# A four-layer graph network in float32: T^T by VectorE, logits and T products in larger batches, z shifted instead of W2 centred, and setup sums moved off TensorE

## Chip, cores and metric

One core of one Trainium2 chip. The metric is the time of one execution on the device, in microseconds (us); medians of several executions are given. All timed runs quoted are of the fast state. "TensorE's clock" is the clock that the throttle granted, 1.00 at full speed.

## The reference, cut to what matters

`x` is 128 graphs of 64 nodes and 512 features, that is 8192 tokens in float32, `adj` the 128 weighted adjacency matrices. Four layers follow, each as `x = x + layer(relu(layernorm(x)), adj)`:

```python
# layer 0: hypergraph convolution 512 -> 1024, relu, layer norm, convolution 1024 -> 512, plus its own input
h = relu(hypergraph_conv(x, adj, W1, b1)); h = layer_norm(h, gamma, beta)
y = hypergraph_conv(h, adj, W2, b2) + x
# layer 1: graph attention with s = (x @ w) @ a, tanh, leaky relu, exp; A @ x @ w
# layer 2: dense attention over the 64 nodes of a graph
query, keyt, value = x @ Wq.T + bq, x @ Wk.T + bk, x @ Wv.T + bv
weight = adj * exp(query @ keyt.T); out = (weight / weight.sum(2)) @ value
# layer 3: diffusion with a transition matrix T from attention
e = leaky_relu(sj[None, :] + si[:, None] + ab); T = normalised(adj * exp(e))
H = sum over k = 0..2 of (T^k @ x) @ Wk[k] + bk[k]; out = relu(H)
```

Some parts of the weights can be worked out once, ahead of the tokens ("setup"): Wq^T Wk for the logits and its bias row, the bias row beta W2 of layer 0, and three vectors (w a, and the two halves of Wv aw) that are then needed in every partition ("spread").

## The kernel before, cut

The kernel works on 16 groups of 512 tokens: first layers 0 and 1 for all groups (first stage), then layers 2 and 3 (second stage). Large products use a seven-product scheme (Strassen's), so VectorE forms sums of blocks beside TensorE. The program first lists all operations, with a cost each, and a list scheduler inside the kernel's own source then fixes the order on each engine. Every transfer goes through one queue, issued by SyncE:

```python
class Graph:
    ENGINES = ("PE", "DVE", "ACT", "POOL", "SP")
    LATENCY = {"PE": 0.30, "DVE": 0.12, "ACT": 0.12, "POOL": 0.15, "SP": 2.0}
    ...
            end = t + o.cost + self.LATENCY[o.eng]      # SP: every transfer is taken to land 2 us after its issue
...
STRETCH, PERIOD1, PERIOD2 = (2.01, 1.52, 3.8, 3.15), 99.32, 100.99
AT = {"x0": -1000.31, "apart": -0.04, "w1": -1140.59, ...}   # priorities of the parts, fitted to that model
```

The parts that the change touches:

```python
def setup_l0():                     # beta W2, and W2 centred: column sums on TensorE
    def mm():
        for c in range(KH):
            nc.tensor.matmul(p.t[0:2, :], gsc[:, c, :], w2_sb[:, c, :], start=(c == 0), stop=(c == KH - 1))
    ...                             # two products that copy the two rows into all partitions (pm, pb)
    for c in range(KH):             # w2 = w2 * gamma - pm
        dve(0.75, ...scalar_tensor_tensor(w2_sb[:, c, :], w2_sb[:, c, :], gb2[:, 0, c:c + 1], pm.t, ...))

def spread(col, dst, r, key):       # a [128, 4] column -> 512 values in every partition
    dve(0.69, lambda: nc.vector.tensor_mul(quad(dg), ident[:, None, :]..., col()[:, :, None]...), r, [dg])
    pe(c_mm(512, 1), lambda: nc.tensor.matmul(p.t, ones, dg.t, start=True, stop=True), [dg], [p])
    act(0.6, lambda: nc.scalar.copy(dst(), p.t), [p], [key])

def dot(in0, in1, acc, r, w):       # a row of h times a spread vector, summed
    j = Buf("o")
    dve(0.77, ...scalar_tensor_tensor(j.t, in0(), 1.0, in1(), ..., accum_out=acc()))

# layer 2: logits of one half as soon as its query block is there: 16 records of 64 columns
pe(c_mm(64, 4), mm, ...)
# layer 3: T^T by TensorE and identity, then T^2, then T products of one tile at a time
for t in range(T):
    nc.tensor.transpose(quad(pt)[:, t, :], tr.t[:, t, :], ident)
act(0.59, lambda: nc.scalar.copy(tt.t[:, :, 0, :], quad(pt)), [pt], [(tt, 0)])
```

## Time and profile before

| | before |
|---|---|
| time, median of 3 runs | 2398.47 us (2397.96 to 2401.6) |
| span of the profiled run, TensorE's clock | 2395.1 us, 0.998 |
| TensorE busy / idle | 2356.3 us / 38.8 us |
| VectorE, ScalarE, GpSimd busy | 1721.2, 1263.5, 938.2 us |
| period (time from one group to the next), first / second stage | 71.77 / 73.20 us |

TensorE is busy 98% of the span. The profile's lines for this, and what follows from them, are shown in the prediction.

### The profile page before, as it was taken

Reading aid. Unit: us, or ns where it says so; the run is one execution under the profiler, and the core shown is the slowest. Engines: PE = TensorE matmul, PEld = TensorE weight load, DVE = VectorE, ACT = ScalarE, POOL = GpSimd, SP = SyncE. Lnnn points to the kernel's source line nnn. Section 1 sums busy time; section 2 is a strip of 40 time slices with the busy share of each in tenths; the row PEclk is TensorE's granted clock in tenths of the full one; section 3 lists DMA queues with packets and bytes.
Section 4 is the critical chain, followed back from the end, with each engine's and each line's share of the span. In section 5 each row is a group of like instructions: output and inputs, shape, how many; then the busy total and the mean of one; then the engine's idle time right before and its main releaser. Section 6 shows DMA issues by size and latency. Waiting matters only on the chain.

```text
span 2395.1 us, 33543 instructions
## 1 busy us (share of the span) xinstructions
PE 2356.3 (98%) x11930; PEld 1855.0 (77%) x11930; DVE 1721.2 (72%) x3676; ACT 1263.5 (53%) x1754; POOL 938.2 (39%) x1450
## 2 busy tenths in 40 slices
PE   7999999999999999999999999999999999999999
PEld 3576677776777776777778888888888888888887
DVE  7887878787878787877878556666666666666664
ACT  2666565566565566565745445544445444454431
POOL 5234455434455434455344333333333333333321
PEclk9999999999999999999999999999999999999999
DMA  7232222232223222222532232222322222222211
GB/s 242 54 80 47 65 68 71 68 78 51 65 66 73 67 80 52 61 67 77 146 89 62 66 74 55 69 56 58 78 64 60 66 50 71 73 56 64 52 42 36
DMA packets 335928, 168.78 MB, mean 70 GB/s; under 512 B 284688, under 2 KB 290832, under 8 KB 335760
## 3 DMA queue, kind: packets, MB, share of 16 engines
q1 hardware_dynamic: 335760, 166.63, 28.0%
q8 instruction: 94, 1.54, 0.3%
q14 instruction: 74, 0.61, 0.1%
HBM read 64.76 MB, written 34.70 MB: 42 GB/s over the span
## 4 chain that ended last, share of the span: by engine, by line
PE 84%; DVE 6%; DMA 4%; ACT 2%; POOL 2%; issue 2%; SPq 0%; DVEq 0%; POOLq 0%; ACTq 0%
PE ps L595 60%; PE ps L818 11%; PE ps L534 4%; PE ps L936 2%; PE ps L731 2%; PE ps L879 2%; DVE s_s_vu_tt L869 1%; DMA x<-xm 1%; PE ps L844 1%; ACT o L543 1%; DVE bd L854 1%; ACT h L525 1%; POOL u L867 1%; POOL rs L511 1%; DVE st L508 1%
## 5 line engine op out<-in xcount | busy, mean ns | idle before, releaser
L525 ACT ACTIVATE h<-x,nm,rs 128x512 f32<-128x512 f32 x384 | 307.1, 813 | 456.5 <-POOL nm L518 455.3
L595 PE MATMUL ps<-wb_mem,rT_a 128*128 128x256 f32 x2056 | 476.8, 380 | 1.7 <-DVE z_hT L615 0.9
L595 PEld LDWEIGHTS ps<-wb_mem,rT_a 128*128 128x128 f32 x2056 | 386.5, 190 | 74.8 <-issue 20.3
L510 POOL TENSOR_SCALAR rs<-mv 128x1 f32<-128x1 f32 x320 | 101.5, 317 | 534.2 <-DVE mv L509 452.9
L595 PE MATMUL ps<-wb_mem,s_s_vu_tt 128*128 128x256 f32 x1152 | 275.0, 379 | 0.2 <-DVE s_s_vu_tt L587 0.2
L595 PE MATMUL ps<-wb_mem,tmp_mB_s 128*128 128x256 f32 x1152 | 261.3, 379 | 0.2 <-DVE tmp_mB_s L587 0.2
L595 PEld LDWEIGHTS ps<-wb_mem,s_s_vu_tt 128*128 128x128 f32 x1152 | 218.5, 190 | 43.1 <-issue 10.5
L595 PE MATMUL ps<-wb_mem,mT_a 128*128 128x256 f32 x1016 | 240.7, 380 | 1.8 <-ACT u L563 1.3
L595 PEld LDWEIGHTS ps<-wb_mem,tmp_mB_s 128*128 128x128 f32 x1152 | 217.6, 190 | 29.6 <-DVE tmp_mB_s L587 0.6
L595 PE MATMUL ps<-wa_mem,mT_a 128*128 128x512 f32 x512 | 238.0, 593 | 2.1 <-DVE u L567 2.1
L949 POOL TENSOR_TENSOR u<-u,bk_b 128x256 f32<-128x256 f32 x96 | 76.2, 799 | 352.3 <-DVE u L567 292.6
L511 POOL TENSOR_TENSOR rs<-rs,mhalf 128x1 f32<-128x1 f32 x320 | 202.9, 634 | 26.6
L595 PEld LDWEIGHTS ps<-wb_mem,mT_a 128*128 128x128 f32 x1016 | 190.6, 190 | 28.6 <-ACT u L563 1.5
L508 DVE BATCH_NORM_STATS2 st<-x 128x6 f32<-128x512 f32 x256 | 174.1, 680 | 32.4 <-DMA x<-xm 30.8
L595 PE MATMUL ps<-wa_mem,s_s_vu_tt 128*128 128x512 f32 x384 | 182.9, 599 | 1.0 <-ACT c_b L453 0.6
L595 PEld LDWEIGHTS ps<-wa_mem,mT_a 128*128 128x128 f32 x512 | 96.0, 190 | 105.4 <-issue 92.5
L565 DVE TENSOR_TENSOR u<-ps,u 128x256 f32<-128x256 f32 (+1 forms) x160 | 84.4, 527 | 112.1 <-PE ps L595 84.6
L623 POOL TENSOR_TENSOR u<-u,row_sh_q 128x256 f32<-128x256 f32 x96 | 70.9, 746 | 235.0 <-DVE u L565 205.9
L545 ACT COPY rT_a<-z_hT 128x1024 uint16<-128x1024 uint16 x128 | 144.3, 1161 | 4.4 <-DMA z_hT<-tmp_mB_s 4.2
L534 PEld LDWEIGHTS ps<-bd,h 128*128 128x128 f32 x1024 | 129.0, 192 | 16.1 <-issue 8.6
L707 ACT ACTIVATE z_hT<-z_hT 128x512 f32<-128x512 f32 x128 | 79.8, 625 | 116.7 <-DVE z_hT L615 116.6
L563 ACT COPY u<-ps 128x256 f32<-128x256 f32 (+1 forms) x160 | 72.5, 453 | 129.7 <-PE ps L818 71.5
(172 smaller groups left out, 4317.1 us busy)
## 6 DMA issues: line engine op xcount, KB each, us to landing
x<-in_x_dram SPq DMA_DIRECT2D x64, 256.0 KB, 2.8
xm<-x SPq DMA_DIRECT2D x64, 256.0 KB, 2.0
x<-xm SPq DMA_DIRECT2D x64, 256.0 KB, 2.7
out_dram<-x SPq DMA_DIRECT2D x64, 256.0 KB, 2.2
adj<-in_adj_dram SPq DMA_DIRECT2D x32, 256.0 KB, 4.1
rw<-row SPq DMA_DIRECT2D x96, 64.0 KB, 2.8
wb_mem<-in_Wk_dram SPq DMA_DIRECT2D x6, 512.0 KB, 4.4
wa_mem<-in_W1T_dram SPq DMA_DIRECT2D x2, 1024.0 KB, 5.9
```

What stands on the lines that cost most here:

```text
L508: dve(0.69, lambda i=i: nc.vector.bn_stats(st.t[:, i, :], src(i)), [r[i]], [(st, i)])
L510: pool(0.3, lambda: nc.gpsimd.tensor_scalar_add(rs.t, mv.t[:, 1:2], EPS), [mv], [rs])
L511: pool(0.65, lambda: nc.gpsimd.tensor_tensor(rs.t, rs.t, mhalf, ALU.pow), [rs], [rs])
L525: act(0.82, lambda: nc.scalar.activation(h.t, xx.t, AF.Relu, bias=nm.t, scale=rs.t), [xx, nm, rs], [h])
L534: nc.tensor.matmul(quad(p)[:, c, :], h.t[:, c * P:(c + 1) * P], rhs(), start=True, stop=True)
L545: act(1.16, lambda: nc.scalar.copy(u16(dst()).rearrange("p c (k q) -> p c k q", q=2), u16(back()).rearrange("p (q c r) -> p c r q", q=2, c ...
L563: act(n / 1200 + 0.17, lambda: nc.scalar.copy(at(0)(), p1.t[:, :n]), [p1], [(U, 0)])
L565: dve(c_v(n), lambda: nc.vector.tensor_add(at(1)(), p2.t[:, :n], at(0)()), [p2, (U, 0)], [(U, 1)])
L595: nc.tensor.matmul(p.t[:, :n], lhs()[:, c, :], rhs(c), start=first and c == 0, stop=c == kc - 1, skip_group_check=True)
L707: act(0.63, lambda: nc.scalar.activation(z.t[:, cols], z.t[:, cols], AF.Relu), [(z, j)], [(z, j)])
L818: nc.tensor.matmul(pair(p.t)[:, o, :], a, b, start=first and o == 0 and c == 0, stop=c == 1, skip_group_check=True)
L949: pool(0.88, lambda: nc.gpsimd.tensor_add(U.t[:, iv], U.t[:, u[1]], add()), [u, ka], [v])
```

## The change

Its intent: take from TensorE what other engines or the queue can do (the transposes of T, the sums in setup, the spreads), batch narrow products so that TensorE changes less often between narrow and full blocks (a full block took 1.92 us between two narrow ones and 1.73 among its own kind), and fit the order anew. The diff, cut to its core:

```diff
-    STRETCH, PERIOD1, PERIOD2 = (2.01, 1.52, 3.8, 3.15), 99.32, 100.99
+    STRETCH, PERIOD1, PERIOD2 = (2.14, 5.21, 2.77, 0.81), 82.23, 144.68
     AT = { ... all offsets new, seven added for the ends of the stages, "last" dropped ... }
 def setup_l0():
-    (column sums of W2 on TensorE, W2 centred by VectorE)
+        acc, pb = Buf("o"), Buf("ps")
+        for c in range(KH):      # beta W2 by VectorE: first c by tensor_scalar, then
+                dve(0.77, lambda c=c: nc.vector.scalar_tensor_tensor(
+                    acc.t, w2_sb[:, c, :], gb2[:, 1, c:c + 1], acc.t, op0=ALU.mult, op1=ALU.add), ...)
+        for c in range(KH):      # W2 * gamma by ScalarE
+            act(0.72, lambda c=c: nc.scalar.activation(w2_sb[:, c, :], w2_sb[:, c, :], AF.Copy, scale=gb2[:, 0, c:c + 1]), ...)
 def spread(col, dst, r, key):
-    (diagonal by VectorE, product with ones by TensorE, copy by ScalarE)
+        d = dram.tile([KD, P], F32, name=f"spread{len(spreads)}")
+        dma(4, lambda: nc.sync.dma_start(d.rearrange("c p -> p c"), col()), r, [k])
+        dma(256, lambda: nc.sync.dma_start(dst(), d.rearrange("c p -> (c p)").partition_broadcast(P)), [k], [key])
 def setup_l2():                  # key bias: Wk^T bq
-            (4 products of one column for each of 4 tiles of Wk)
+                dve(0.77, ...scalar_tensor_tensor(bk.t, k_.t, bq_c[:, o:o + 1], bk.t, ...))   # then 4 products at the end
 layer 0:                         # z shifted by its mean, W2 no longer centred
-    act(0.7, ...activation(half(), half(), AF.Copy, scale=rs.t))
+    nm = offset(mv, rs)          # GpSimd
+    act(0.72, ...activation(half(), half(), AF.Identity, bias=nm.t, scale=rs.t))
 layer 2:                         # logits of two query blocks together
-    pe(c_mm(64, 4), mm, ...)
+    pe(1.5, mm, ...)             # 32 records
 layer 3:
-    nc.tensor.transpose(quad(pt)[:, t, :], tr.t[:, t, :], ident); act copy
+    nc.vector.transpose(tt.t[... 32 rows ...], tr.t[... 32 columns ...])     # 8 a group
-    pe(c_mm(128, KD) + 0.2, lm, ...)            # T products of one tile
+    pe(2 * c_mm(128, KD) + 0.25, lm, ...)       # of two tiles, four PSUM banks
```

## The prediction

> **What bounds the kernel now.** I read the engine totals and the 40 slices first, then busy time by stretches, TensorE's groups by form, TensorE's waits, and TensorE's timeline of one steady period.
>
> ```profile
> PE 2356.3 (98%) x11930; PEld 1855.0 (77%) x11930; DVE 1721.2 (72%) x3676; ACT 1263.5 (53%) x1754; POOL 938.2 (39%) x1450
> PE   7999999999999999999999999999999999999999
> DVE  7887878787878787877878556666666666666664
> ...
> 0.00:20.00 20.00, 10.48 (x24) 5.06 (x25) 10.66 (x23) 2.10 (x2) 5.04 (x15) 1.00 0.78 279
> ...
> 400.00:640.00 240.00, 240.00 (x1000) 170.85 (x999) 189.92 (x420) 149.19 (x210) 113.18 (x176) 1.00 0.26 65
> ...
> 1180.00:1240.00 60.00, 55.22 (x312) 45.73 (x311) 40.02 (x85) 23.43 (x33) 21.07 (x37) 1.00 0.48 130
> ...
> 1640.00:1880.00 240.00, 239.06 (x1441) 205.90 (x1440) 153.03 (x313) 110.96 (x150) 83.02 (x128) 1.00 0.27 65
> ```
>
> The columns of the stretches are length, then busy time of TensorE, weight load, VectorE, ScalarE, GpSimd, then clock and DMA. TensorE has work without a gap in both long stages; VectorE, the next, is busy 79% of the first (layers 0 and 1) and 64% of the second (layers 2 and 3). Of the 2395.1 us, 38.8 are idle on TensorE: 16.6 in the first 100 us (9.5 of them before the first matmul), 9.9 at the handover between stages (1150 to 1290), some 7.6 in the last 105 us, and the rest are 0.3 us waits. So only two things change the time: TensorE's own work, and these gaps.
>
> Busy time of matmuls overlaps in this profile, so I cost by start-to-start distance. The recurring order of instructions gives 71.77 us a group of 512 tokens in the first stage (230.81 to 302.58 in the chain) and 73.20 in the second (1330.76 to 1403.95); the 16 groups make 1148 and 1171 us, and 76 us are left for setup, edges and gaps.
>
> ```profile
> L844 PE MATMUL ps<-y_qT,z_hT 128*64 128x64 f32 x1024 | 44.7, 231 | 1.4 <-ACT y_qT L830 1.3
> L915 PE MATMUL ps<-ident,bd 128*128 128x128 f32 x64 | 9.8, 275 | 1.9 <-DVE bd L908 1.9
> L435 PE MATMUL ps<-wb_mem,gsc 128*2 128x512 f32 x16 | 7.0, 592 | 0.0
> L474 PE MATMUL ps<-bq_c,tmp_mB_s 128*128 128x1 f32 x32 | 3.7, 242 | 0.0
> L452 PE MATMUL ps<-tmp_mB_s,ones 128*128 128x512 f32 x6 | 3.2, 622 | 0.1
> ```
>
> These are the groups that the change touches: logits, transposes of T, and three setup products. An ordinary matmul counts as two records here. The next lines are TensorE's timeline, first in the steady second stage and then once at the handover:
>
> ```profile
> 1645.35 3.62 PE L818 MATMUL ps<-row_sh_q,wa_mem 128*128 128x256 f32 x16
> 1648.89 0.69 PE L844 MATMUL ps<-y_qT,z_hT 128*64 128x64 f32 x16
> 1649.51 1.99 PE L818 MATMUL ps<-wa_mem,row_sh_q 128*128 128x256 f32 x8
> 1651.43 0.69 PE L844 MATMUL ps<-y_qT,z_hT 128*64 128x64 f32 x16
> 1652.05 1.99 PE L818 MATMUL ps<-z_hT,wa_mem 128*128 128x256 f32 x8
> ...
> 1205.82 1.89 PE L818 MATMUL ps<-wa_mem,row_sh_q 128*128 128x256 f32 x8
> 1207.64 1.15 PE L844 MATMUL ps<-y_qT,z_hT 128*64 128x64 f32 x32
> 1208.72 1.99 PE L818 MATMUL ps<-z_hT,wa_mem 128*128 128x256 f32 x8
> 1210.55 1.89 PE L818 MATMUL ps<-wa_mem,row_sh_q 128*128 128x256 f32 x8
> ```
>
> A block of 8 products of 256 columns takes 1.73 us from start to start among its own kind (1669.07 to 1670.80), but 1.92 between two blocks of logits. A switch into and out of a narrow block therefore costs 0.19 us outside the block, besides something inside it.
>
> [...] the trace has 216 ns a record for 256 columns of float32, [...] and I use 216. [...] No VectorE transpose is in this trace.
>
> **The change part by part.**
> Transposes of T: four records at 1614.17, the next kind at 1614.61, so 0.44 us a group go from TensorE, in 16 groups 7.0 us. ScalarE loses one 0.585 us eviction a group. VectorE gains eight transposes of 32 rows by 128: its 512 and 256 column operations take 0.69 and 0.42 us, so 128 columns should take 0.28, together 2.3 us a group (an estimate). That raises it from 64% to 67%: beside the path.
>
> Second power of T: half the columns, but 65 columns (8 records in 0.84 us at 485.67) cost nearly what 128 do (0.89): nothing gained.
>
> Logits in pairs: one block of 16 records costs 0.62 + 0.19 = 0.81 us, one of 32 costs 1.08 + 0.19 = 1.27. A pair saves 0.35. In steady state all four of a group stood apart, so 0.70 a group, 11 us in all, less a little for the groups where they already touched.
>
> T products in pairs of tiles: a block of 16 records takes 1.09 us, of 32 1.98, of 48 2.88, that is 0.9 for each 16 and 0.19 for a block. But the scheduler already placed them as 16 + 48 in each group; 32 + 32 is two blocks too. No gain, and four PSUM banks are held at once.
>
> Setup: column sums of W2 (L435) 6.96 us from start to start, one selecting product 0.96 and the 0.69 wait for its row; the key bias has 32 records at 0.11, of which 8 stay, minus 2.6; the three spreads minus 2.6. That is 13.1 us of work and 0.7 of wait, replaced by two transfers a spread, about 8 VectorE operations more for the bias row and key bias, and 8 ScalarE scalings of W2.
>
> z shifted instead of W2 centred: 64 more GpSimd operations of 0.466 us, 30 us beside a queue at 49%; the shift is the bias of an activation that ran anyway. It adds 0.5 us of latency before each pair of transposed tiles, which other layers' work covers in the long stages.
>
> New order: the first stage's 71.77 us are already TensorE's work without a gap (its products add up to 71.6), so no schedule can gain there. At the ends it can: the Wq and Wk tiles now go ahead of W1, and W2 far later. Before, the first matmul waited to 9.5 us for Wk behind 2 MB of W1, with DMA 78 to 96% busy; with only 1 MB ahead I estimate 5 us. Handover and tail have new offsets of their own; I give them 4 and 1, and 1 for the 15 waits of 0.3 us for the reciprocal.
>
> The sum: 7.0 + 11 + 13.1 + 0.7 = 31.8 of work; plus about 10 of gaps; less 1 to 2 for a hole that the freed setup work leaves while VectorE, over 90% busy between 40 and 80 us, still prepares the first tiles. 2398.5 minus about 41 is **2357 us**.
>
> **The rivals.**
> A, *the setup gain evaporates*: TensorE waits at 63, 74 and 84 us for VectorE, not for itself; if VectorE sets the end of setup, the 13 us removed there turn into idle time and VectorE's added operations lengthen it. For it: VectorE's load between 40 and 80 us. Against: from 28 us the combined tiles were ready, and setup products ran to 41.9 in front of the first layer product. Then about 2369.
> B, *the edges gain more*: with the offsets searched anew for start, handover and end, most of the 34 us at the edges close to half. For it: the added offsets aim at just that, and there is mixed work to fill with. Against: the first loads and the last chain cannot be hidden. Then about 2345.
> C, *a new wait in the second stage*: paired logits hold both query buffers and delay two PSUM evictions, paired T products need four banks. If each group gains one 0.7 us wait, the logit gain is gone: about 2368. Against it: TensorE always has two layers' work to choose from there.
>
> **Range and chances.** The mechanical part (transposes, logits, setup) is 32 us, and I hold it to within 6; the edges are worth 0 to 22. So 2340 to 2374 eight times in ten. The limit for faster by over 2% is 2350.5, some 7 us below my centre, reached if B holds: 0.33. Slower by over 2% would need 48 us of new waits where TensorE has none: 0.01. Within 2%: 0.66.
>
> **What would show it.** Right: no record of an identity transpose; about 32 logit blocks of 32 records each, two a group; a second-stage period of 72.1 us against 73.2 and a first-stage period of 71.8 as before; first matmul near 5 us; idle time of TensorE near 29 us. VectorE's transposes at about 0.28 us. Wrong: a second-stage period still at 73, then C; idle time in the first 100 us above 20 us, then A; idle time in all under 20 us, then B. Most likely to spoil the figure is the size of the gaps at the edges, which comes from a schedule that I can't see.

## The result and the profile after

| | before | after |
|---|---|---|
| time, median (runs, same rounds) | 2400.03 us (4) | 2410.00 us (4; 2409.17 to 2411.19) |
| span of the profiled run, clock | 2395.1 us, 0.998 | 2409.4 us, 0.989 |
| TensorE busy / idle | 2356.3 / 38.8 us | 2337.8 / 71.6 us |

The ratio is 1.0041, with a 95% interval of 1.0024 to 1.0058. A ratio here is the mean time of one kernel's fast runs over the mean of the other's of the same rounds, so it is not quite the ratio of the medians. The change costs some 10 us where I had predicted a gain of 41. TensorE did lose work, and lost more to waiting.

From the page of after, the totals and the slices:

```profile
PE 2337.8 (97%) x11818; PEld 1851.6 (77%) x11818; DVE 1763.9 (73%) x3801; ACT 1267.6 (53%) x1742; POOL 965.9 (40%) x1514
...
PE   7689999999999999999999999999999999999998
...
DVE  7778878877888787787867667766667766667763
```

The hole is in slices 2 and 3, that is between 60 and 180 us, where before had 9s. To say how much each stage gives or takes, I compare the moments at which the same products start in both traces:

| from ... to | before | after | difference |
|---|---|---|---|
| start to the 16th group's product of the first stage with the adjacency | 1059.8 us | 1085.7 | +25.9 |
| to the second group's T squared | 264.3 | 266.0 | +1.6 |
| to the 15th group's (13 periods) | 952.7 | 934.6 | -18.1 |
| to the 16th group's | 69.2 | 73.8 | +4.6 |
| to the end | 49.1 | 49.4 | +0.3 |

The differences are taken before rounding; their sum, +14.3, is the difference of the two spans. **The second stage gained as intended, and the start of the program lost more.** The period of the first stage is 71.77 us in both, so nearly all of the 25.9 arises before about 180 us.

The second stage first. TensorE's groups by form of after (busy time in us and mean ns):

```profile
L850 PE MATMUL ps<-y_qT,z_hT 128*64 128x64 f32 x1024 | 37.3, 225 | 1.6 <-DVE y_qT L835 1.6
...
L932 PE MATMUL ps<-s_s_vu_tt,bd 128*128 128x64 f32 x128 | 18.0, 288 | 8.5 <-DVE s_s_vu_tt L923 8.5
```

The identity transposes are gone. The logits take 37.3 us of busy time in place of 44.7. TensorE's timeline of a steady stretch of after (start, length, then line and operands):

```profile
1744.81 1.15 PE L850 MATMUL ps<-y_qT,z_hT 128*64 128x64 f32 x32
1745.89 1.99 PE L817 MATMUL ps<-z_hT,wa_mem 128*128 128x256 f32 x8
1747.72 1.89 PE L817 MATMUL ps<-wa_mem,row_sh_q 128*128 128x256 f32 x8
1749.54 1.15 PE L850 MATMUL ps<-y_qT,z_hT 128*64 128x64 f32 x32
```

Two blocks of 32 records a group, 1.08 us each from start to start, as predicted.

Now the start. The stretches of after (length; busy TensorE, weight load, VectorE, ScalarE, GpSimd; clock, DMA share, GB/s):

```profile
0.00:20.00 20.00, 10.61 (x24) 5.02 (x24) 7.08 (x25) 1.65 (x2) 4.68 (x16) 1.00 0.83 292
20.00:40.00 20.00, 14.35 (x46) 7.52 (x46) 19.65 (x17) 10.73 (x17) 18.07 (x14) 0.91 0.67 231
40.00:60.00 20.00, 19.36 (x51) 9.40 (x51) 16.82 (x29) 6.13 (x11) 1.57 (x4) 0.83 0.50 173
60.00:80.00 20.00, 9.54 (x31) 4.72 (x29) 13.64 (x38) 8.80 (x11) 6.45 (x16) 0.93 0.73 65
80.00:100.00 20.00, 12.40 (x47) 9.16 (x48) 13.38 (x21) 8.21 (x11) 9.08 (x7) 0.81 0.59 128
```

TensorE is idle 100 - 66.26 = 33.7 us of the first 100, against 16.6 before. The granted clock falls as well, to 0.81 between 80 and 100 us. TensorE's timeline of after (in brackets: idle before, and what ended it):

```profile
72.16 1.99 PE L593 MATMUL ps<-wb_mem,rT_a 128*128 128x256 f32 x8 [2.94 <-ACT rT_a L543]
83.75 3.78 PE L593 MATMUL ps<-wb_mem,rT_a 128*128 128x256 f32 x8 [9.60 <-ACT u L561]
```

After the hole of 2.94 us a block of 8 records takes its usual 1.99 us, at a granted clock of 1.00 (72.16 to 73.90 us); after the one of 9.60 it takes 3.78, at 0.50 (83.75 to 87.50 us). So more was lost there than the hole's own length: the block behind it took 1.79 us longer.

What TensorE waited for in after, in all the run (total us, times, longest):

```profile
PE ps L593 <- ACT u L561: 9.6, 1, 9.6
PE ps L593 <- DVE mT_a L585: 8.8, 1, 8.8
PE ps L932 <- DVE s_s_vu_tt L923: 8.5, 2, 6.8
PE ps L459 <- DMA tmp_mB_s<-in_Wk_dram: 7.1, 1, 7.1
...
PE ps L434 <- DVE o L430: 4.3, 1, 4.3
```

The first is said to wait for ScalarE. What kept ScalarE? Its own timeline says: a transposing transfer.

```profile
82.14 1.16 ACT L543 COPY rT_a<-z_hT 128x1024 uint16<-128x1024 uint16 x1 [9.09 <-DMA z_hT<-tmp_mB_s]
83.32 0.37 ACT L561 COPY u<-ps 128x256 f32<-128x256 f32 x1
```

And the timeline of the queue that issues all transfers at that time:

```profile
69.22 0.48 SPq L442 DMA_DIRECT2D spread<-col  x1
69.80 0.48 SPq L319 DMA_DIRECT2D tmp_mB_s<-in_aw_dram  x1
70.39 3.21 SPq L542 DMA_TRANSPOSE z_hT<-tmp_mB_s  x2
80.30 0.33 SPq L443 DMA_DIRECT2D c_b<-spread  x1
80.69 1.24 SPq L542 DMA_TRANSPOSE z_hT<-tmp_mB_s  x1
```

The spread is written at 69.22 and read back at 80.30, as soon as the write has landed; until then the queue stands still. It is tempting to say that the transposing transfer behind the read-back was what ScalarE lacked. But that one, issued at 80.69, landed only at 86.44, after ScalarE had gone on at 82.14. ScalarE had waited for the transfer issued at 70.39, before the queue stood still, which landed at 82.12. The transposing transfers of this stretch, with their times from issue to landing (minimum/median/maximum), first in after, then in f6, a run described below in which, up to this point, only the layout of the spread's write differs:

```profile
L542 SPq DMA_TRANSPOSE z_hT<-tmp_mB_s x3: 1295/1352/1823, 67.7 to 71.8; - x3
DMA to landing us min/median/max: 3.2/10.6/11.7
```

```profile
z_hT<-tmp_mB_s SPq DMA_TRANSPOSE x2, 4.0
```

The transfer issued just before the write took 3.2 us; a load of 256 KB issued right behind it took 11.4, and the two transposing transfers after that 11.7 and 10.6. In f6 that load takes 3.6 and those two 4.0 in the median. So transfers that were in flight together with this write landed late, then ScalarE went on late, then TensorE. What in the write holds the others up, no run shows. The spread's transfers by name, and the queue's own waits, in after:

```profile
spread<-col SPq DMA_DIRECT2D x3, 2.0 KB, 10.9
```

```profile
SPq L443 <- DMA spread<-col: 25.0, 3, 10.3
```

Three writes of 2 KB land after 10.9 us in the median, and the queue stands for 25.0 us in all. The write goes to `d.rearrange("c p -> p c")`, so neighbouring elements of the source lie 512 bytes apart in memory: 512 pieces of 4 bytes. The packet counts agree: the queue moved 338496 packets in after and 337344 in f6, which writes 128 pieces of 16 bytes, and the 1152 between them are 3 x (512 - 128). Other transfers of the same 2 KB (`row<-col`) land after 1.4 us.

The second wait in the list (8.8 us, for VectorE) has the same root by another way: there VectorE waits for the write and then for its read-back. VectorE's timeline of after at the third spread, 150 us into the run:

```profile
138.70 0.37 DVE L585 TENSOR_TENSOR s_s_vu_tt<-s_s_vu_tt,mT_a 128x256 f32<-128x256 f32 x1
149.34 0.69 DVE L373 SCALAR_TENSOR_TENSOR o<-h,row_sh_q 128x512 f32<-128x512 f32 x1 [10.27 <-DMA row_sh_q<-spread]
...
150.57 0.42 DVE L585 TENSOR_TENSOR mT_a<-mT_a 128x256 f32<-128x256 f32 x1
```

VectorE stands 10.27 us before its first use of the spread vector, and the block sum of line 585, which TensorE needs, stands behind that use in VectorE's own order.

There is a second suspect, earlier. VectorE's timeline of after:

```profile
28.78 1.54 DVE L430 SCALAR_TENSOR_TENSOR o<-wb_mem,gb,o 128x512 f32<-128x512 f32 x2
...
30.36 8.58 DVE L430 SCALAR_TENSOR_TENSOR o<-wb_mem,gb,o 128x512 f32<-128x512 f32 x5
38.86 1.48 DVE L585 TENSOR_TENSOR s_s_vu_tt<-mT_a 128x256 f32<-128x256 f32 x1
```

Five of the new sums take 1.7 us each, where the first two took 0.77. GpSimd's timeline of the same stretch:

```profile
30.42 2.95 POOL L694 TENSOR_TENSOR x<-x,h 128x512 f32<-128x512 f32 x2
33.33 6.73 POOL L695 TENSOR_TENSOR x<-x,row_sh_q 128x512 f32<-128x512 f32 x4
```

The slow sums ran beside these additions of 512 columns, the two quick ones beside operations of one column. TensorE waits 4.3 us for the last of them (line 434 in its list of waits), and the first block sums of layer 0 (line 585) stand behind them. That they stood side by side is all that the trace shows: no run here isolates it, so the cause of the slowness is not shown.

### The profile page after: what moved, and what is told of

It reads as the page before. It is cut to its first block, busy times and chain, and to the rows that moved or that the text cites. A ratio compares the mean times of both kernels' runs of the same rounds, so it can differ in the third digit from the quotient of the medians.

```text
span 2409.4 us, 33461 instructions
## 1 busy us (share of the span) xinstructions
PE 2337.8 (97%) x11818; PEld 1851.6 (77%) x11818; DVE 1763.9 (73%) x3801; ACT 1267.6 (53%) x1742; POOL 965.9 (40%) x1514
## 2 busy tenths in 40 slices
DMA packets 338665, 170.88 MB, mean 71 GB/s; under 512 B 286400, under 2 KB 292544, under 8 KB 338496
## 3 DMA queue, kind: packets, MB, share of 16 engines
q1 hardware_dynamic: 338496, 168.74, 29.8%
## 4 chain that ended last, share of the span: by engine, by line
PE 86%; DVE 3%; DMA 2%; ACT 1%; POOL 1%; issue 0%; SPq 0%; DVEq 0%; POOLq 0%
PE ps L593 58%; PE ps L817 15%; PE ps L532 4%; PE ps L886 2%; PE ps L730 2%; PE ps L948 2%; PE ps L850 1%; DMA x<-xm 1%; DVE st L502 1%; PE ps L932 0%; DMA rw<-row 0%; PE ps L677 0%; ACT tmp_mB_s L541 0%; ACT rT_a L543 0%; ACT z_hT L717 0%
## 5 line engine op out<-in xcount | busy, mean ns | idle before, releaser
L523 ACT ACTIVATE h<-x,nm,rs 128x512 f32<-128x512 f32 x384 | 300.1, 809 | 403.3 <-POOL nm L510 378.7
L504 POOL TENSOR_SCALAR rs<-mv 128x1 f32<-128x1 f32 x320 | 95.0, 297 | 506.5 <-DVE mv L503 490.5
L593 PE MATMUL ps<-wa_mem,mT_a 128*128 128x512 f32 x512 | 241.1, 604 | 10.9 <-DVE mT_a L585 8.8
L505 POOL TENSOR_TENSOR rs<-rs,mhalf 128x1 f32<-128x1 f32 x320 | 196.0, 612 | 26.5
L510 POOL TENSOR_SCALAR nm<-mv,rs 128x1 f32<-128x1 f32 x320 | 138.8, 434 | 31.1
```

The source lines that it names most:

```text
L504: pool(0.32, lambda: nc.gpsimd.tensor_scalar_add(rs.t, mv.t[:, 1:2], EPS), [mv], [rs])
L505: pool(0.65, lambda: nc.gpsimd.tensor_tensor(rs.t, rs.t, mhalf, ALU.pow), [rs], [rs])
L510: pool(0.47, lambda: nc.gpsimd.tensor_scalar(nm.t, mv.t[:, 0:1], rs.t, -1.0, op0=ALU.mult, op1=ALU.mult), [mv, rs], [nm])
L523: act(0.82, lambda: nc.scalar.activation(h.t, xx.t, AF.Relu, bias=nm.t, scale=rs.t), [xx, nm, rs], [h])
L593: nc.tensor.matmul(p.t[:, :n], lhs()[:, c, :], rhs(c), start=first and c == 0, stop=c == kc - 1, skip_group_check=True)
```

## The experiments

Two theories of the lost start, by the names that the recorded expectations use: **Q**, the slow write of the spread; **S**, the sums on VectorE ahead of the block sums. Q was recorded with a path, that the in-order queue stands still and holds up the transposing transfers behind it; the layout of the write and that path are tested apart below. The rival is **O**, the new order itself (offsets).

Any change of the operations makes the scheduler produce another order. So the runs named e... are whole versions with an order of their own, and those named f... keep after's order of all instructions on all engines and change one thing in it.

**e1, e2, e3, e4: the spread on TensorE again, its landing time told to the scheduler, the spread in runs, the sums on TensorE again.** Edits, each against after:

```diff
 e1: spread() as in the kernel before
 e2:
-    dma(4, lambda: nc.sync.dma_start(d.rearrange("c p -> p c"), col()), r, [k])
+    dma(4, lambda: nc.sync.dma_start(d.rearrange("c p -> p c"), col()), r, [k], lat=11.0)
-            end = t + o.cost + self.LATENCY[o.eng]
+            end = t + o.cost + o.lat
 e3:
-    d = dram.tile([KD, P], F32); write to d.rearrange("c p -> p c"); read d.rearrange("c p -> (c p)") into dst
+    d = dram.tile([P, KD], F32)                   # 16 bytes of each partition together
+    dma(4, lambda: nc.sync.dma_start(d, col()), r, [k])
+    dma(256, lambda: nc.sync.dma_start(b.t, d.rearrange("p c -> (p c)").partition_broadcast(P)), [k], [b])
+    act(0.72, lambda: nc.scalar.copy(dst()..."q (c p) -> q c p"..., b.t..."q (p c) -> q c p"...), [b], [key])
 e4: beta W2 and the key bias by TensorE as in the kernel before (W2 neither centred nor scaled by VectorE)
```

> The changed kernel, but the three spreads (a column of 4 values in each of 128 partitions, made into a row of 512 in all of them) go through TensorE again as before, not through DRAM. Changed kernel 2410, kernel before 2400. Theory Q (queue): the write of a spread takes about 10 us to land because it goes out in 4-byte pieces, and the queue's next instruction, the read back, waits at the head of the in-order queue and holds up the transposing transfers behind it; TensorE runs dry for 9.6 us and its clock halves. Then the three waits (25 us in all on the queue) vanish, TensorE's idle time in the first 160 us falls from 45 to under 30 us, and the time to about 2392. Theory S (sums): the setup sums now on VectorE hold up the first tiles; then under 4 us change, 2407. Theory O (order): the new order of loads and tiles is what is slow; then under 5 us, either way.

> The changed kernel with the same instructions, but the scheduler in the program is told that the write of a spread lands after 11 us and not after 2, so it should put other transfers between write and read. Theory Q: the queue's wait for the spreads falls from 25 us to under 5, the time to about 2396, a little worse than with TensorE's spread [...]. Theories S and O: 2405 to 2410, though the queue's wait falls too.

> The changed kernel, the spread still through DRAM but written in runs of 16 bytes (partition order), read back by all partitions, and put in order by one ScalarE copy. Theory Q: the write lands in about 1.5 us as the other small columns do (1.4 us), the queue's wait nearly vanishes, the time about 2392, as with TensorE's spread. If the 512 pieces are not the cause of the slow landing, it still takes about 10 us and the time stays near 2410.

> The changed kernel with the sums of setup (bias row of layer 0, key bias of layer 2) on TensorE as before; spreads stay through DRAM. Theory S: VectorE is free of 12 operations that took up to 1.7 us each between 27 and 39 us, the first combined tiles come about 10 us sooner, and TensorE's added 10 us lie in holes: about 2400. Theory Q: TensorE gets 10 us more work, holes shrink by some: 2405 to 2415. Theory O: as Q.

| run | median, us | before, same rounds | ratio to before (95%) |
|---|---|---|---|
| e1_spread_pe | 2396.74 | 2399.01 | 0.9987 (0.9978 to 0.9996) |
| e2_spread_known | 2406.55 | 2399.01 | 1.0033 (1.0021 to 1.0045) |
| e3_spread_runs | 2394.17 | 2399.01 | 0.9979 (0.9971 to 0.9987) |
| e4_sums_pe | 2397.87 | 2399.01 | 0.9994 (0.9988 to 1.0001) |

Undoing the spread alone (e1), mending it (e3), or undoing the sums alone (e4) each brings after back to the time of before or a little below, some 12 to 16 us. Telling the scheduler the true landing time (e2) was expected to bring 2396 if Q held; it helped little, though the queue's wait for the spread fell from 25.0 to 8.0 us. That miss speaks against the path in Q. In e2's trace the queue goes on issuing behind the first write, and still the transposing transfers issued after it land only after 9.7 to 10.2 us, and TensorE has a hole of 7.2 us at the same place. All four runs have orders of their own, so they don't yet give each cause its size.

**f3, f4, f5: the same in after's order.** f3 writes the spread in 16-byte runs and lets the readers take the vector in its mixed order; f4 leaves the VectorE sums out (their result is zero in this data, since beta and bq are zero; it is no usable kernel); f5 does both.

```diff
 f3:
-    dma(4, lambda: nc.sync.dma_start(d.rearrange("c p -> p c"), col()), r, [k])
+    dma(4, lambda: nc.sync.dma_start(d, col()), r, [k])          # d is [P, KD]
-    dot(lambda h=h: h.t, lambda s=s: c3_b[:, s, :], ...)
+    dot(lambda h=h: h.t.rearrange("q (c p) -> q c p", c=KD), lambda s=s: c3_b[:, s, :].rearrange("q (p c) -> q c p", c=KD), ...)
 f4:
-    dve(0.77, lambda c=c: nc.vector.scalar_tensor_tensor(acc.t, ...
+    dve(0.77, lambda c=c: None and nc.vector.scalar_tensor_tensor(acc.t, ...
```

> The changed kernel with every engine's order of instructions kept as it is: only the spread's write goes out in runs of 16 bytes (partition order), and the readers look at the row through a strided view instead of a copy. This takes the order out of the comparison, which the first four runs could not. Theory Q: the write lands in 1.5 to 2 us, the queue's 25 us of waits fall to about 5, the 9.6 us hole of TensorE goes, and the time is 2392 to 2398, as in the run with runs of 16 bytes and a new order (2394). If that run owed its gain to its new order, this one stays above 2405. [...]

> The changed kernel in its own order with the ten scalar_tensor_tensor sums of setup on VectorE left out (both sums are of zeros in these inputs, so the result stays right; it is no kernel to use). Theory S: the first combined tiles come up to 10 us sooner, TensorE's 4.3 us wait for the bias row goes, and the time is 2398 to 2402. If the sums lie beside other waits of the start: 2407 or more.

> Both of the above in the changed kernel's own order. If the two losses are separate holes, their gains add up: about 2385 (15 and 10 us below 2410). If removing one only uncovers the other, about 2393, no better than the better one alone.

| run | median, us | before, same rounds | ratio to before (95%) |
|---|---|---|---|
| f3_runs_same_order | 2417.47 | 2399.04 | 1.0079 (1.006 to 1.0098) |
| f4_sums_gone | 2399.58 | 2399.04 | 1.0004 (0.9994 to 1.0014) |
| f5_both_same_order | 2416.67 | 2399.04 | 1.0075 (1.0058 to 1.0091) |

f4 gives S its size in after's order: about 10 us. f3 and f5 missed what was expected of them, and the trace shows that the experiment was spoilt, so that it decides nothing about Q. VectorE's instructions on the spread vector, first in after, then in f3 (minimum/median/maximum ns):

```profile
L373 DVE SCALAR_TENSOR_TENSOR o<-h,c_b x128: 658/689/1091, 1267.2 to 2346.4; 128x512 f32<-128x512 f32 x128
```

```profile
L373 DVE SCALAR_TENSOR_TENSOR o<-h,c_b x128: 1052/1096/1518, 1248.6 to 2353.9; 128x512 f32<-128x512 f32 x128
```

Reading with a step of 16 bytes costs VectorE 0.41 us more (1096 ns against 689) for each of 128 instructions in the second stage, far more than I had guessed, at the head of layer 3's chain; there T squared now waits for VectorE in every group (16.0 us in all). The start itself was mended: the first of these instructions begins at 1248.6 in place of 1267.2. So the second stage had to be freed of the strided reads.

**f6, f7: again, with the row put in order once.** Two VectorE copies at the first use of each row, through a buffer that this use holds anyway; the order of instructions is after's. f7 leaves the sums out as well (as f4).

```diff
-    dve(0.77, lambda: nc.vector.scalar_tensor_tensor(j.t, in0(), 1.0, in1(), ...
+    dve(0.77, lambda: in_order(key, j) or nc.vector.scalar_tensor_tensor(j.t, in0(), 1.0, in1(), ...
+    def in_order(key, j):
+        if key in mixed:
+            row = mixed.pop(key)()
+            nc.vector.tensor_copy(j.t.rearrange("q (c p) -> q c p", c=KD), row.rearrange("q (p c) -> q c p", c=KD))
+            nc.vector.tensor_copy(row, j.t)
```

> The same test as f3, mended. There the first 160 us lost 23 us less than in the changed kernel, but the strided readers cost 0.41 us each on VectorE (1096 ns against 689) in every group and made the second stage slower. Here every engine's order is again the changed kernel's own; the write goes out in runs of 16 bytes, and at its first use each row is put in order once on VectorE (two copies), so that the readers are as before. Theory Q: the loss of the start falls as in f3, the second stage keeps its 71.6 us a group, the time is 2390 to 2396. Theory that the order of the earlier run (2394) was the gain: 2405 or more.

> f6 with the ten sums of setup on VectorE left out too (zeros in these inputs; not a kernel to use). Alone they gave 10 us (2399.6 against 2410). If the losses of the spread and of the sums are separate: 2381 to 2386. If one covers the other: 2390 or more.

f6 took 2390.95 us beside 2401.34 for before, a ratio of 0.9956 (0.994 to 0.9971); f7 took 2384.37, a ratio of 0.993 (0.9914 to 0.9946). The transfers by name, and TensorE's waits in the first 180 us, of f6:

```profile
spread<-col SPq DMA_DIRECT2D x3, 2.0 KB, 2.3
```

```profile
PE ps L468 <- DMA tmp_mB_s<-in_Wk_dram: 6.8, 1, 6.8
PE ps L541 <- ACT h L532: 6.4, 2, 3.6
PE ps L434 <- DVE o L430: 4.3, 1, 4.3
```

Both waits of about 9 us of after are gone, with nothing altered but where the 2 KB are laid and the three rows put in order. **That the write's layout costs this time is shown**: 4-byte pieces against 16-byte runs, 10.9 against 2.3 us to landing, in the same order, is worth some 20 us of the whole. (The two were not run side by side; their ratios to before, 1.0041 and 0.9956, are 0.0085 apart.) The path, late landing of what was in flight beside the write, is read from the traces of after, f6 and e2. With the layout mended, taking the sums away is worth another 6.6 us (f6 to f7), where alone they were worth 10. By the times, that overlap is within the noise; the traces agree with it: the 16th group's product of the first stage starts at 1085.7 us in after, 1073.5 in f4, 1062.1 in f6 and 1055.8 in f7, so the sums are worth 12.2 us of the start alone and 6.3 on top of f6.

**e5 and e6: both mended, in a usable kernel.** e3 and e4 together; e6 is the same kernel once more, beside e8.

> A usable version of both: sums of setup on TensorE as before, spreads in runs of 16 bytes with a ScalarE copy, order from the scheduler anew. Theories Q and S together: 2385 to 2390, better than the kernel before by about 12; TensorE does 10 us more setup work than in the run with both removed, some of it in holes. The tail's hole of 6.8 us stays.

> e5_sums_pe_runs again, beside e8_tuned on the same chip: 2390 us, ratio 0.996 to the kernel before.

e5 took 2390.05 us beside 2399.04 (ratio 0.9962, 0.9949 to 0.9975); e6 2392.80 beside 2400.81 (0.9973, 0.9964 to 0.9982). It gives correct results and beats both kernels by a little.

**e8: e5 with the order fitted anew.** The kernel's scheduler returns its own reckoning of the time, in which every transfer lands in 2 us. It says 2373.6 for before and 2356.2 for after: a gain of 17 where the chip showed a loss. The offsets were fitted to a reckoning that missed what spoilt them. For e8 they were searched again against a replay with durations nearer to the traces; the operations are e5's.

```diff
-    AT = {"x0": -1295.17, "apart": -2.73, "w1": -1120.0, "b1": -878.71, "w2": 35.83, "w": 372.04, "c1": -986.57, ...}
+    AT = {"x0": -1197.52, "apart": 125.7, "w1": -837.14, "b1": -939.23, "w2": -90.55, "w": 537.16, "c1": -1045.23, ...}
```

> The operations of e5_sums_pe_runs, with the offsets that fix the order of instructions searched anew against a replay of the program's own scheduling in which a transfer lands in 2.5 us and VectorE and ScalarE take the times of the traces. The replay gives 2377 us for these offsets and 2389 for e5's. Theory (what is left of the loss at the start is order fitted to wrong durations): 2376 to 2382 us, a ratio of 0.990 to 0.993 against the kernel before. Rival (the replay is no better a guide than the program's own model, whose gain of 17 us the chip turned into a loss of 10): within 5 us of e5's 2390, either way. The replay gave 2378 for f6_runs_same_order2, which took 2391, so I lean to the rival.

e8 took 2382.82 us beside 2400.81 for before, a ratio of 0.9934 (0.992 to 0.9949), 10 us below e6 on the same chip. I had leaned to the rival there, and that was wrong: the time is more than 5 us from e5's. The theory came nearer, and just missed its range (2376 to 2382): the replay had promised 12. It is the fastest usable version of this study. Three of its stretches, and its longest wait of TensorE in all the run (total, times, longest):

```profile
20.00:40.00 20.00, 20.00 (x71) 9.04 (x70) 11.54 (x26) 5.53 (x9) 9.70 (x12) 1.00 0.91 322
40.00:60.00 20.00, 14.55 (x47) 7.60 (x46) 16.46 (x29) 11.30 (x19) 12.10 (x14) 0.91 0.74 211
60.00:80.00 20.00, 20.00 (x70) 11.14 (x69) 16.90 (x41) 13.80 (x19) 6.03 (x9) 1.00 0.48 85
```

```profile
PE ps L927 <- DVE s_s_vu_tt L918: 8.5, 2, 6.8
...
```

From 20 to 80 us TensorE is idle 5.5 us (60 - 54.55) where after was idle 16.8 (60 - 43.25). That does not bring the start forward as a whole: e8's 16th group's product of the first stage stands at 1060.6 us, before's at 1059.8. e8's 16.3 us (spans of 2378.8 and 2395.1) are 17.6 in the 13 periods of the second stage and 3.2 at the handover, less 0.7 at the start and 3.7 at the end. The hole before the last T squared stays in e8.

## Why the prediction was wrong, point by point

- **What bounds it** (TensorE's work and its gaps): right. The loss is exactly in those gaps.
- **Transposes of T, 7.0 us; logits, 11 us**: right. TensorE's work, counted with the start-to-start cost of each kind of instruction, falls by some 20 us, of which 7 are transposes and 13 setup; this count leaves out what a switch of form costs (0.19 us outside the block, from the 1.92 and 1.73 of the prediction), so the logits' 11 show only in the period. The second stage's period was predicted at 72.1 and is typically 71.61 (71.89 in the mean of 13 groups).
- **T products in pairs, "No gain"**: wrong, in the good direction. The two pairs of a group now stand as one block of 64 records, which takes 3.77 us, where 16 + 48 took 1.09 + 2.88 = 3.97 by the durations in the prediction: 0.2 us a group. With 0.44 for the transposes, 0.70 for the logits and 0.3 for the wait for the reciprocal, which is gone, that is 1.64 against the 1.59 measured (73.20 - 71.61). The prediction had counted those waits of 0.3 us, one in nearly every group, as 1 us in all.
- **VectorE's transposes at 0.28 us**: eight took 2.52 us, 0.31 each. Beside the path in the steady stage, as said.
- **First matmul near 5 us**: 7.1, from 9.5. About half of the gain.
- **Setup, 13.1 us of work and 0.7 of wait "replaced by two transfers a spread, about 8 VectorE operations more"**: this is the step that failed. The work did go (13 us). But the replacements were priced at nothing. The write of a spread lands after 10.9 us, transfers right behind it after 10.6 to 11.7, and its read-back stands in VectorE's order ahead of block sums that TensorE needs: some 20 us (f6). The sums stand there too: 10 us alone (f4), 7 with the spread mended (f7). It is their place that costs and not their number: VectorE has 125 operations more, which are the 128 transposes less 3, so setup has 3 fewer and not 8 more. With the first matmul I had the start at about -17 (13.1 + 0.7 + 4.5, less 1 to 2); it came to +25.9. That is 43 of the 53 us by which the prediction missed (2410 - 2357).
- **Rival A** set the mark "idle time in the first 100 us above 20 us", and 33.7 us met it. Its reason, VectorE, was the smaller part (S: 7 to 10 us); its time, 2369, was far too low. The larger cause, the layout of the write, was in none of my rivals.
- **Rivals B and C**: neither sign came. TensorE's idle time is 71.6 us and not under 20, and the second stage's period is not at 73.
- **z shifted, GpSimd "at 49%"**: the line shown has 113.18 of 240 us, 47%. Nothing hangs on it.
- **Handover 4, tail 1**: neither gain came. The handover came to +1.6; in e8, with offsets of its own, it is -3.2 (1060.6 to 1321.7). The tail came to +4.9, the sum of the last two rows.

The tail's chain in after:

```profile
2350.49 2.75 PE L593 MATMUL ps<-wb_mem,tmp_mB_s 128*128 128x256 f32 x12
2360.03 1.97 PE L932 MATMUL ps<-s_s_vu_tt,bd 128*128 128x64 f32 x8 [6.79 <-DVE s_s_vu_tt L923]
2362.47 6.31 PE L948 MATMUL ps<-s_s_vu_tt,h 64*128 64x128 f32 x64 [0.46 <-ACT s_s_vu_tt L934]
```

In the last group no other group's work is left to stand in while VectorE finishes T and transposes it: a hole of 6.8 us, then T squared in 1.97 us at a granted clock of 0.50, then 64 records in 6.31 us in place of 3.77, at 0.58 in the mean of that block (0.50 up to 2365.5 us, 0.66 after). Before had W3 products of the previous group (12 + 24 + 12 records) up to its T squared. Whether this hole comes from the new chain over VectorE or from the order alone was not tested; it stays open.

Even with both causes away (f7), the predicted 17 us of the start don't appear. f7 reaches the 16th group's product of the first stage at 1055.8 us, before at 1059.8, only 4 sooner, and gives that back at the handover: it reaches the second group's T squared at 1325.2, before at 1324.1. Yet its work is some 21 us less than before's in all. e8, with its sums on TensorE, carries some 9 us more of TensorE work than f7 and is as fast. This suggests that TensorE's work does not set the length of the setup here, and that transfers, VectorE and ScalarE do; that much of rival A's premise would hold. It is argued and not shown, since f7 and e8 differ in order too. What of the remaining chain is loads and what is block sums I did not separate.

## What to carry to other kernels

Before moving work from a busy engine to a queue or another engine, ask in that very stretch which engine TensorE waits for, and what comes behind the new operation, in flight beside it or in an engine's order: three 2 KB writes cost some 20 us because transfers and block sums behind them were late. A long wait of the issuing queue is not yet the cause: see which transfer the waiting engine needed, and when that one was issued. Lay a small write so that the memory side has runs (here 2 KB landed after 10.9 us in pieces of 4 bytes and after 2.3 in runs of 16), and look at the time from issue to landing of small transfers too. An order fitted to a reckoning of durations is only as good as these durations; after a change of operations, compare them with the trace before believing the fitted gain.
